# Two graph attention layers on one core: when the four logits of a step end in the order's model, and layer 0's products in parts of two key blocks

## The chip, the core and the metric

The kernel runs on one core of a Trainium2 chip. The time is device time in microseconds of one execution. A profile is one more execution, taken by the hardware profiler.

## The reference

x holds 16 graphs of 1024 nodes with 256 features, adj their adjacency (0 or 1, about 3% ones). Two layers follow each other; behind each one the result is added to x and normalized row by row.

Layer 0 has 4 heads of 64 features. The reference:

```python
h = jnp.einsum('bnd,hde->bhne', nodes_embed, W)
weight = weight + mask * (e_src[:, :, t, :, None] + e_dst[:, :, t, None, :])
weight = jax.nn.leaky_relu(weight, negative_slope=0.01)
weight = jnp.where(node_adj[:, None] == 0, NEG, weight)
attention = jax.nn.softmax(weight, axis=-1)
dst = jnp.einsum('bhij,bhje->bhie', attention, h) + bias[None, :, None, :]
out = jax.nn.relu(dst) + h          # then a normalization of each head's 64 features
```

Layer 1 has 8 heads of 32 features. Queries, keys and values are all the same normalized rows:

```python
scores = jnp.einsum('bhqd,bhkd->bhqk', qkv, qkv) * scale
masked = jnp.where(mask, scores, -jnp.inf)
attn = jax.nn.softmax(masked, axis=-1)
out = jnp.einsum('bhqk,bhkd->bhqd', attn, qkv)
x = x + out                         # then y = layer_norm(x)
mlp = jax.nn.gelu(y @ W1 + b1, approximate=False) @ W2 + b2
```

## The kernel before

**Two streams and one order.** Layer 0 of a graph and layer 1 of the graph before it share the engines. Each layer is a Python generator (layer0 and layer1, lines 941 to 983) that issues instructions and then yields a number of units of work and the things that it needs next. The loop at lines 1007 to 1023 picks, at each turn, which of the two goes on. What it picks sets the order of the instructions in the queues of TensorE (PE), VectorE (DVE), ScalarE (ACT) and GpSimd (POOL); on the chip each of these queues is worked off in that order. All instructions pass through a helper at line 61, so all of them have that line in the profile, and groups are told apart by the names of their tiles.

**How the loop picks.** A whole layer 0 of a graph is WORK0 = 47 units: 13 for prepare, 2 at the start of attention0, 32 for its products. A whole layer 1 is WORK1 = 138 units: 82 for attention (ATTN1), 56 for the mlp. COURSE says how far layer 0 should be (in graphs, ahead of layer 1's graph) when layer 1 has done so many units: 1.0 at its start, 1.42 at unit 82, 2.0 at unit 128 and after. Layer 0 goes on while it is behind this target. The choice is turned round if the stream that was picked is late by 0.3 us more than the other, as long as layer 0 stays within SLACK = 0.06 graphs (2.8 units) of the target, and no further ahead than 2.05 graphs (lines 1011 to 1016).

**Where lateness comes from.** Class Pace (lines 90 to 167) keeps a model of the chip while the program is built: for each engine when it is free, for each tile when it was last written and read. enter() puts an instruction at the latest of these and adds a cost; a matmul of a 32x128 tile over 512 columns is 0.22 us in it. The four such matmuls of a step start one after the other in the model. written of a tile is the end of its matmul plus 0.2. Ring.ready() gives when the oldest buffers of a ring come free.

**Layer 0.** prepare (line 481) loads two blocks of 128 rows at a time, turns them (tiles xk, xT), turns the adjacency (ak) to a mask of bytes (ACT, Square), and projects (w0e). Since a logit of layer 0 is a sum of a term of the query and one of the key, exp of the leaky sum is a maximum of two products; spread_factor (line 558) spreads the query's term over all partitions with matmuls into two of the four ps banks and copies them to cb by ACT; weights (line 569) makes p0 by one DVE instruction for each key block of 128 keys and 512 queries. products (line 586) multiplies p0 with the values in 128x64 tiles, 8 matmuls for a key block, each with two records in the profile. A step of attention0 is a head, a half of the queries and four of the eight key blocks: 64 records, named acc<-v,p. Its weights are two p0 tiles; ring "four" has four such buffers, and weights of step i+1 are issued behind the products of step i. spread_factor for the next pair of heads is issued in the first step of a pair's second head.

**After layer 0.** residual0 and after0 (lines 626 to 717) are chains: generators that go on in advance() when what they need is ready in the model. after0 normalizes per head, then per row; its ACT instruction sq<-hb,t,r makes the normalized rows, and PE and ACT turn them into nT, that is layer 1's queries and keys.

**Layer 1.** exponentials (line 729) makes a step's four logits: four matmuls of 32x128 tiles (records ps<-nT, eight a step) into the four banks of the ring ps_s, and four exponentials on ACT into two p tiles. masked multiplies them with the mask on DVE. products (line 748) does two heads as "moved" (po<-p,v and po<-p,unit) and two as "held" (po<-v,p), three steps behind the logits (LAG). There are 32 steps a graph. The mlp (line 858) goes over four chunks of 256 rows: first() is ps<-yT,w_sb and a gelu on ACT, second() is po<-w_sb,hid; one unit of the order is two first() or half a second(), 1.75 each.

The step loop of attention0 as it stands:

```python
steps = [(n, hd, j4) for n in range(NH) for hd in range(H0) for j4 in range(0, NB, 4)]
...
            products(ps, hd, j4, av)
            advance()
            if i + 1 < len(steps):
                ps = weights(*steps[i + 1])
```

Of the kernel before, what the change touches and what calls it, by code (L numbers as in the profile page):

```python
# [31 lines left out]
F32 = mybir.dt.float32  # L32
# [4 lines left out]
OP = mybir.AluOpType  # L37
PSUM = bass.MemoryType.PSUM

P = 128  # L40
# [49 lines left out]
class Pace:  # L90
# [20 lines left out]
    def through(self, tile):  # L111
        return max(self.written.get(tile, 0.0), self.read.get(tile, 0.0))

    def now(self):
        return self.free["tensor"]

# [54 lines left out]
def fast_path(  # L171
# [24 lines left out]
    nc = Pace(tc.nc)  # L196
    B, N, D = x.shape
    H0, _, HO = w0.shape
# [4 lines left out]
    NB = N // P  # L203
    DC = D // P
    FC = DFF // P
    HALF = 512
    NH = N // HALF
    BPH = HALF // P
    Q = 32
    TILE = 64  # L210
    PAIR = 2
    GB = 2
    QUAD = 4
# [337 lines left out]
    def attention0(b, hb, v0, esr, dinv, factors, mask, rinv):  # L551

        groups = [(n, pair) for n in range(NH) for pair in range(H0 // PAIR)]
        steps = [(n, hd, j4) for n in range(NH) for hd in range(H0) for j4 in range(0, NB, 4)]

        def spread_factor(n, pair):

            cb = two.tile([P, PAIR, HALF], F32, name="cb")  # L560
            pbs = [ps_s.tile([P, HALF], F32, name="ps") for _ in range(PAIR)]
            for e in range(PAIR):
                q = slice((pair * PAIR + e) * Q, (pair * PAIR + e + 1) * Q)
                nc.tensor.matmul(pbs[e], spread[q, :], esr[q, n * HALF : (n + 1) * HALF], start=True, stop=True)
            for e in range(PAIR):
                nc.scalar.copy(cb[:, e, :], pbs[e])
            return cb

        def weights(n, hd, j4):
            ps = []  # L570
            cb = cbs[n, hd // PAIR]
            for j2 in (j4, j4 + 2):
                p = four.tile([P, 2, HALF], F32, name="p0")
                for i in range(2):
                    nc.vector.scalar_tensor_tensor(
                        p[:, i, :],
                        cb[:, hd % PAIR, :],
                        dinv[:, j2 + i, hd : hd + 1],
                        mask[n][:, j2 + i, :],
                        op0=OP.max,  # L580
                        op1=OP.mult,
                    )
                ps.append(p)
            return ps

        def products(ps, hd, j4, av):
            for i in range(4):
                for q in range(BPH):
                    for at in range(0, P, TILE):
                        nc.tensor.matmul(  # L590
                            av[at : at + TILE, q, :],
                            ps[i // 2][:, i % 2, q * P + at : q * P + at + TILE],
                            v0[:, j4 + i, hd, :],
                            start=j4 + i == 0 and q == 0,
                            stop=j4 + i == NB - 1 and q == BPH - 1,
                        )

        cbs = {groups[0]: spread_factor(*groups[0])}
        yield 1.0,
        nc.vector.tensor_copy(factors, v0[:, :, :, HO])  # L600
        ps = weights(*steps[0])
        yield 1.0, bank0_ready, *ps
        for i, (n, hd, j4) in enumerate(steps):
            if j4 == 0:
                av, bank = bank0([P, BPH, HO + 1])
                bank["busy"] = True
            products(ps, hd, j4, av)
            advance()
            if i + 1 < len(steps):
                ps = weights(*steps[i + 1])  # L610
            if j4 == 0 and i + 3 < len(steps) and hd % PAIR == PAIR - 1:
                g = steps[i + 3][0], steps[i + 3][1] // PAIR
                cbs[g] = spread_factor(*g)
            if j4 == NB - 4:
                h = hb[n][:, :, hd * HO : (hd + 1) * HO]
                residual = residual0(av, h, rinv[:, n * BPH : (n + 1) * BPH, hd])
                residuals[b, n, hd] = residual
                bank["busy"] = False
                bank["readers"] = [residual]
                begin(residual, "vector", av)  # L620
                if hd % PAIR == PAIR - 1:
                    norms[b, n, hd] = after0(b, n, hd, hb[n])
                    begin(norms[b, n, hd], "vector", done(residual), hb[n])
            yield (2.0, *ps, *([bank0_ready] if j4 == NB - 4 else []))

    def residual0(av, h, rinv):

# [92 lines left out]
    def attention1(half, mask, rinv, half_done):  # L720

        steps = [(n, quad, jb) for n in range(NH) for quad in range(H1 // QUAD) for jb in range(NB)]

        def exponentials(n, quad, jb):
            keys = slice(jb % BPH * P, (jb % BPH + 1) * P)  # L730
            of_keys, of_queries = half(jb // BPH)[2], half(n)[2]
            tiles = [ps_s.tile([P, HALF], F32, name="ps") for _ in range(QUAD)]
            for e in range(QUAD):
                q = slice(e * HD, (e + 1) * HD)
                nc.tensor.matmul(tiles[e], of_keys[q, quad, keys], of_queries[q, quad, :], start=True, stop=True)
            ps = []
            for e in range(0, QUAD, PAIR):
                p = eight.tile([P, PAIR, HALF], F32, name="p")
                for i in range(PAIR):
                    nc.scalar.activation(p[:, i, :], tiles[e + i], AF.Exp, scale=SCALE1)  # L740
                ps.append(p)
            return ps

        def masked(n, quad, jb, ps):
            for p in ps:
                nc.vector.tensor_mul(p, p, mask[n][:, jb, None, :].to_broadcast([P, PAIR, HALF]))

        def products(quad, jb, ps, moved, held):
            values = half(jb // BPH)[1][:, jb % BPH, :, :]
            for e in range(PAIR):  # L750
                hd = quad * QUAD + e
                for at, v in ((e, values[:, hd, 0:HD]), (PAIR + e, unit)):
                    nc.tensor.matmul(
                        moved[at * Q : (at + 1) * Q, :], v, ps[0][:, e, :], start=jb == 0, stop=jb == NB - 1
                    )
            for e in range(PAIR):
                hd = quad * QUAD + PAIR + e
                for q in range(BPH):
                    for at in range(0, P, Q):
                        nc.tensor.matmul(  # L760
                            held[at : at + Q, q, e, :],
                            ps[1][:, e, q * P + at : q * P + at + Q],
                            values[:, hd, :],
                            start=jb == 0 and e == 0 and q == 0,
                            stop=jb == NB - 1 and e == PAIR - 1 and q == BPH - 1,
                        )

        LAG = 3
        ready = {}

        def logits_ready():
            return ps_s.ready("ps", QUAD)

        def outs_ready():
            return ps_o.ready("po", 2)

        for i in range(len(steps) + LAG):
            if i < len(steps):
                ready[i] = exponentials(*steps[i])
                advance()  # L780
            if 0 <= i - 1 < len(steps):
                masked(*steps[i - 1], ready[i - 1])
                advance()
            if i < LAG:
                yield 1.0, logits_ready
                continue
            n, quad, jb = steps[i - LAG]
            if jb == 0:
                moved = ps_o.tile([P, HALF], F32, name="po")
                held = ps_o.tile([P, BPH, PAIR, HD + 1], F32, name="po")  # L790
            products(quad, jb, ready.pop(i - LAG), moved, held)
            if jb == NB - 1:
                if quad == 0:
                    o = one.tile([P, BPH, D], F32, name="o0")
                chain = heads_out(n, quad, moved, held, o, rinv)
                begin(chain, "vector", held, moved, o)
                if quad == H1 // QUAD - 1:
                    half_done(n, o, chain)
            yield (2.5, logits_ready, *ready.get(i - LAG + 1, ()), *([outs_ready] if jb == NB - 1 else []))
# [185 lines left out]

    WORK0 = NB // GB * 3.25 + 2.0 + NB * H0 // 2 * 2.0
    ATTN1 = 2.0 + 2.5 * (NH * NB * H1 // QUAD)
    WORK1 = ATTN1 + NB // GB * (1.75 * FC / 2 + 3.5 * GB)  # L990
    SLACK = 0.06
    COURSE = [(0.0, 1.0), (ATTN1, 1.42), (WORK1 - 10.0, 2.0), (WORK1, 2.0)]

    def wanted():
        b, done = place[1]
# [11 lines left out]
    while any(streams):  # L1007
# [9 lines left out]
        step = next(streams[which], None)  # L1017
# [453 lines left out]
```

## Time and profile before

| | us |
|---|---|
| median of 3 runs | 3573.72 (3570.82 to 3583.27) |
| profiled execution | 3564.78 |
| its span, first to last instruction | 3563.0 |
| PE busy | 3443.4 (97%) |
| DVE busy | 2989.8 (84%) |
| ACT busy | 2010.2 (56%) |
| mean granted clock of PE | 0.983 |

The costliest groups, with count, busy us and mean ns: exponentials on ACT (p<-ps, 2048, 1061.0, 616); masking on DVE (p<-p,mask, 1024, 1188.9, 1217); logits on PE (ps<-nT, 4096 records, 794.6, 651); layer 0's weights on DVE (p<-cb,dinv,mask, 1024, 698.9, 743); layer 0's products on PE (acc<-v,p, 16384 records, 547.6, 225). Matmuls overlap in these rows: busy time is the time in which at least one is under way, and their ends are modelled. The distance from the start of one group to the start of the next is what a group takes of PE.

The first graph's layer 0 runs alone until about 115 us, and the last graph's layer 1 runs alone from about 3384 us. Between them a graph takes some 217 us. In the timeline a row is a run of like instructions: start, length, engine, line, operation, tiles, shapes, count, and in brackets the idle time before it with what ended it.

### The profile page before, as it was taken

The numbers are of one execution on the slowest core, as the hardware profiler recorded it, in microseconds if no ns is written. First come the engines' busy times: TensorE is split into PE (matmuls) and PEld (weight loads), VectorE is DVE, ScalarE is ACT, GpSimd is POOL, SyncE is SP. The second block draws the span as 40 slices with busy tenths as digits, with TensorE's granted clock in tenths as the row PEclk, the third lists the DMA queues.
The fourth block names the chain that finished last, engine by engine and source line by source line (L and its number), as shares of the span: only waits on it lengthen the run. The fifth ranks groups of instructions, "written<-read, shape, count | busy, mean of one in ns | idle before, by whom it ended". The sixth has DMA issues, their size and how long they took to land.

```text
span 3563.0 us, 141472 instructions
## 1 busy us (share of the span) xinstructions
PE 3443.4 (97%) x64417; PEld 2329.2 (65%) x64417; DVE 2989.8 (84%) x5267; ACT 2010.2 (56%) x4320; POOL 413.7 (12%) x424
## 2 busy tenths in 40 slices
PE   6799999999999999999999999999999999999998
PEld 4458576675856658576585766757567585765846
DVE  5888898988888888898888979888798888988883
ACT  2564746547375563845647466474654737556373
POOL 0102011010110101011020110101101011010100
PEclk9899999999999999999999999999999999999999
DMA  4111101011020110201111010110201102010000
GB/s 107 32 20 34 30 14 41 12 34 30 16 45 9 37 24 17 47 12 35 21 30 33 13 39 15 34 30 14 41 13 33 30 16 45 9 37 9 16 6 14
DMA packets 77809, 97.51 MB, mean 27 GB/s; under 512 B 9104, under 2 KB 60048, under 8 KB 77200
## 3 DMA queue, kind: packets, MB, share of 16 engines
q0 software_dynamic: 18432, 33.56, 6.4%
q1 hardware_dynamic: 57184, 53.76, 5.0%
q8 instruction: 506, 8.29, 1.0%
q10 hardware_dynamic: 1584, 1.05, 0.1%
q14 instruction: 103, 0.84, 0.1%
HBM read 105.13 MB, written 16.78 MB: 34 GB/s over the span
## 4 chain that ended last, share of the span: by engine, by line
PE 91%; ACT 5%; DVE 2%; issue 1%; DMA 0%; POOL 0%; ACTq 0%; POOLq 0%; DVEq 0%
PE po L61 36%; PE ps L61 34%; PE acc L61 21%; ACT p L61 2%; DVE p L61 1%; ACT sq L61 1%; ACT mask L61 1%; ACT xT L61 0%; ACT z L61 0%; DMA w0e<-in_L_gnn_W_dram 0%; DVE hb L61 0%; ACT cb L61 0%; ACT hb L61 0%; POOL r L61 0%; DVE z L61 0%
## 5 line engine op out<-in xcount | busy, mean ns | idle before, releaser
L61 ACT ACTIVATE p<-ps 128x512 f32<-128x512 f32 x2048 | 1061.0, 616 | 417.3 <-PE ps L61 417.3
L61 DVE TENSOR_TENSOR p<-p,mask 128x1024 f32<-128x1024 f32 x1024 | 1188.9, 1217 | 27.0 <-ACT p L61 26.8
L61 PE MATMUL ps<-nT 32*128 32x512 f32 x4096 | 794.6, 651 | 12.3 <-ACT cb L61 9.8
L61 DVE SCALAR_TENSOR_TENSOR p<-cb,dinv,mask 128x512 f32<-128x512 f32 x1024 | 698.9, 743 | 23.3 <-ACT cb L61 23.3
L61 PEld LDWEIGHTS po<-v,p 128*32 128x32 f32 x32768 | 398.6, 110 | 317.0 <-issue 264.8
L61 ACT ACTIVATE hid<-ps,b_sb 128x256 f32<-128x256 f32 x512 | 242.5, 474 | 639.6 <-PE ps L61 639.6
L61 PE MATMUL acc<-v,p 128*64 128x65 f32 x16384 | 547.6, 225 | 18.3 <-DVE p L61 16.3
L61 PEld LDWEIGHTS acc<-v,p 128*64 128x64 f32 x16384 | 507.9, 139 | 83.6 <-issue 38.8
L61 PE MATMUL po<-p,v 128*32 128x512 f32 x2048 | 553.5, 615 | 0.0
L61 PE MATMUL po<-p,unit 128*32 128x512 f32 x2048 | 553.1, 615 | 0.0
L61 PE MATMUL ps<-yT,w_sb 128*128 128x256 f32 x2048 | 478.4, 383 | 0.0
L61 PE MATMUL po<-w_sb,hid 128*128 128x256 f32 x2048 | 474.6, 384 | 0.0
L61 PEld LDWEIGHTS po<-w_sb,hid 128*128 128x128 f32 x2048 | 381.7, 190 | 64.8 <-issue 11.4
L61 PEld LDWEIGHTS ps<-yT,w_sb 128*128 128x128 f32 x2048 | 380.3, 190 | 62.9 <-issue 11.4
L61 PEld LDWEIGHTS ps<-nT 32*128 32x128 f32 x4096 | 286.2, 186 | 166.2 <-ACT p L61 56.8
L61 PE MATMUL po<-v,p 128*32 128x33 f32 x32768 | 390.5, 198 | 4.4 <-issue 4.4
L61 PEld LDWEIGHTS po<-p,v 128*32 128x32 f32 x2048 | 78.7, 109 | 340.0 <-issue 210.8
L61 POOL TENSOR_TENSOR r<-v,mhalf 128x1 f32<-128x1 f32 (+1 forms) x192 | 152.8, 801 | 842.0 <-DVE v L61 493.0
L61 DVE TENSOR_TENSOR z<-acc,bias_r 128x256 f32<-128x256 f32 x128 | 54.1, 423 | 200.0 <-ACT hb L61 200.0
L61 POOL TENSOR_TENSOR r<-v1s,mhalf 128x4 f32<-128x4 f32 x32 | 61.7, 1927 | 1092.9 <-DVE v1s L61 1092.9
L61 POOL DMA_DIRECT2D ak<-in_adj_dram x128 | 69.7, 545 | 976.9 <-PE acc L61 963.1
L61 PE MATMUL acc<-w0e,xT 128*128 128x264 f32 x512 | 149.3, 415 | 20.0 <-issue 10.4
(109 smaller groups left out, 2909.4 us busy)
## 6 DMA issues: line engine op xcount, KB each, us to landing
ak<-in_adj_dram POOLq DMA_DIRECT2D x128, 256.0 KB, 3.9
xk<-in_x_dram SPq DMA_DIRECT2D x64, 256.0 KB, 2.8
xl<-in_x_dram SPq DMA_DIRECT2D x32, 512.0 KB, 3.9
out_dram<-z SPq DMA_DIRECT2D x128, 128.0 KB, 1.7
w_sb<-in_L_gnn_W_dram SPq DMA_DIRECT2D x2, 1024.0 KB, 6.7
v<-in_L_gnn_a_src_dram SPq DMA_DIRECT2D x2, 320.0 KB, 4.4
v<-in_L_gnn_a_dst_dram ACTq DMA_DIRECT2D x1, 320.0 KB, 6.5
xl<-in_L_gnn_a_dst_dram ACTq DMA_DIRECT2D x1, 320.0 KB, 7.8
```

Source lines behind the costliest of these rows:

```text
L61: return method(*args, **kwargs)
```

## The change

The model gets a method, together(), which sets the model's read and written times of several tiles to the latest among them. exponentials calls it ahead of a step's four logits and behind them. It issues no instruction. Layer 0's products go in parts of two key blocks (32 records) for one unit each, in place of four key blocks for two units; the weights of three parts are made before the first products, and those of part i+3 are issued behind the products of part i. spread_factor for the next pair is issued in the first part of a pair's second head, four parts ahead of the first that belongs to the next pair. COURSE asks for 1.38 in place of 1.42 at the end of attention, and for 2.0 from 14 units before the end, in place of 10. WORK0 stays 47.

```diff
--- before.py
+++ after.py
@@ -110,6 +110,12 @@
 
     def through(self, tile):
         return max(self.written.get(tile, 0.0), self.read.get(tile, 0.0))
+
+    def together(self, tiles):
+
+        names = [t.tensor.name for t in tiles]
+        for times in (self.read, self.written):
+            times.update(dict.fromkeys(names, max(times.get(name, 0.0) for name in names)))
 
     def now(self):
         return self.free["tensor"]
@@ -208,6 +214,7 @@
     BPH = HALF // P
     Q = 32
     TILE = 64
+    AHEAD = 3
     PAIR = 2
     GB = 2
     QUAD = 4
@@ -553,7 +560,7 @@
 
 
         groups = [(n, pair) for n in range(NH) for pair in range(H0 // PAIR)]
-        steps = [(n, hd, j4) for n in range(NH) for hd in range(H0) for j4 in range(0, NB, 4)]
+        steps = [(n, hd, j) for n in range(NH) for hd in range(H0) for j in range(0, NB, PAIR)]
 
         def spread_factor(n, pair):
 
@@ -566,52 +573,50 @@
                 nc.scalar.copy(cb[:, e, :], pbs[e])
             return cb
 
-        def weights(n, hd, j4):
-            ps = []
+        def weights(n, hd, j):
             cb = cbs[n, hd // PAIR]
-            for j2 in (j4, j4 + 2):
-                p = four.tile([P, 2, HALF], F32, name="p0")
-                for i in range(2):
-                    nc.vector.scalar_tensor_tensor(
-                        p[:, i, :],
-                        cb[:, hd % PAIR, :],
-                        dinv[:, j2 + i, hd : hd + 1],
-                        mask[n][:, j2 + i, :],
-                        op0=OP.max,
-                        op1=OP.mult,
-                    )
-                ps.append(p)
-            return ps
-
-        def products(ps, hd, j4, av):
-            for i in range(4):
+            p = four.tile([P, PAIR, HALF], F32, name="p0")
+            for i in range(PAIR):
+                nc.vector.scalar_tensor_tensor(
+                    p[:, i, :],
+                    cb[:, hd % PAIR, :],
+                    dinv[:, j + i, hd : hd + 1],
+                    mask[n][:, j + i, :],
+                    op0=OP.max,
+                    op1=OP.mult,
+                )
+            return p
+
+        def products(p, hd, j, av):
+            for i in range(PAIR):
                 for q in range(BPH):
                     for at in range(0, P, TILE):
                         nc.tensor.matmul(
                             av[at : at + TILE, q, :],
-                            ps[i // 2][:, i % 2, q * P + at : q * P + at + TILE],
-                            v0[:, j4 + i, hd, :],
-                            start=j4 + i == 0 and q == 0,
-                            stop=j4 + i == NB - 1 and q == BPH - 1,
+                            p[:, i, q * P + at : q * P + at + TILE],
+                            v0[:, j + i, hd, :],
+                            start=j + i == 0 and q == 0,
+                            stop=j + i == NB - 1 and q == BPH - 1,
                         )
 
         cbs = {groups[0]: spread_factor(*groups[0])}
         yield 1.0,
         nc.vector.tensor_copy(factors, v0[:, :, :, HO])
-        ps = weights(*steps[0])
-        yield 1.0, bank0_ready, *ps
-        for i, (n, hd, j4) in enumerate(steps):
-            if j4 == 0:
+
+        ps = [weights(*step) for step in steps[:AHEAD]]
+        yield 1.0, bank0_ready, ps[0]
+        for i, (n, hd, j) in enumerate(steps):
+            if j == 0:
                 av, bank = bank0([P, BPH, HO + 1])
                 bank["busy"] = True
-            products(ps, hd, j4, av)
+            products(ps.pop(0), hd, j, av)
             advance()
-            if i + 1 < len(steps):
-                ps = weights(*steps[i + 1])
-            if j4 == 0 and i + 3 < len(steps) and hd % PAIR == PAIR - 1:
-                g = steps[i + 3][0], steps[i + 3][1] // PAIR
-                cbs[g] = spread_factor(*g)
-            if j4 == NB - 4:
+            if i + AHEAD < len(steps):
+                ps.append(weights(*steps[i + AHEAD]))
+            if j == 0 and i + NB // PAIR < len(steps) and hd % PAIR == PAIR - 1:
+                n1, hd1, _ = steps[i + NB // PAIR]
+                cbs[n1, hd1 // PAIR] = spread_factor(n1, hd1 // PAIR)
+            if j == NB - PAIR:
                 h = hb[n][:, :, hd * HO : (hd + 1) * HO]
                 residual = residual0(av, h, rinv[:, n * BPH : (n + 1) * BPH, hd])
                 residuals[b, n, hd] = residual
@@ -621,7 +626,7 @@
                 if hd % PAIR == PAIR - 1:
                     norms[b, n, hd] = after0(b, n, hd, hb[n])
                     begin(norms[b, n, hd], "vector", done(residual), hb[n])
-            yield (2.0, *ps, *([bank0_ready] if j4 == NB - 4 else []))
+            yield (1.0, *ps[:1], *([bank0_ready] if j == NB - PAIR else []))
 
     def residual0(av, h, rinv):
 
@@ -730,9 +735,12 @@
             keys = slice(jb % BPH * P, (jb % BPH + 1) * P)
             of_keys, of_queries = half(jb // BPH)[2], half(n)[2]
             tiles = [ps_s.tile([P, HALF], F32, name="ps") for _ in range(QUAD)]
+
+            nc.together(tiles)
             for e in range(QUAD):
                 q = slice(e * HD, (e + 1) * HD)
                 nc.tensor.matmul(tiles[e], of_keys[q, quad, keys], of_queries[q, quad, :], start=True, stop=True)
+            nc.together(tiles)
             ps = []
             for e in range(0, QUAD, PAIR):
                 p = eight.tile([P, PAIR, HALF], F32, name="p")
@@ -985,11 +993,11 @@
 
 
 
-    WORK0 = NB // GB * 3.25 + 2.0 + NB * H0 // 2 * 2.0
+    WORK0 = NB // GB * 3.25 + 2.0 + NB * H0 * 1.0
     ATTN1 = 2.0 + 2.5 * (NH * NB * H1 // QUAD)
     WORK1 = ATTN1 + NB // GB * (1.75 * FC / 2 + 3.5 * GB)
     SLACK = 0.06
-    COURSE = [(0.0, 1.0), (ATTN1, 1.42), (WORK1 - 10.0, 2.0), (WORK1, 2.0)]
+    COURSE = [(0.0, 1.0), (ATTN1, 1.38), (WORK1 - 14.0, 2.0), (WORK1, 2.0)]
 
     def wanted():
         b, done = place[1]
```

## The prediction

> **What bounds the kernel now.** I first read the page's head: TensorE (PE) is busy 97% of the span, VectorE (DVE) 84%, ScalarE (ACT) 56%.
>
> ```profile
> span 3563.0 us, 141472 instructions
> PE 3443.4 (97%) x64417; PEld 2329.2 (65%) x64417; DVE 2989.8 (84%) x5267; ACT 2010.2 (56%) x4320; POOL 413.7 (12%) x424
> ...
> PE 91%; ACT 5%; DVE 2%; issue 1%; DMA 0%; POOL 0%; ACTq 0%; POOLq 0%; DVEq 0%
> ```
>
> The chain of waits agrees: PE 91%. But 97% isn't PE at its peak. So second I read the timeline of one graph in the middle of the run (1643 to 1861 us; others look alike) and took, for each group of matmuls, the distance to the start of the next. A logits step (8 records of ps<-nT, four matmuls of 32 rows side by side) usually takes 1.07 us:
>
> ```profile
> 1668.62 1.14 PE L61 MATMUL ps<-nT 32*128 32x512 f32 x8
> 1669.69 0.62 PE L61 MATMUL po<-p,v 128*32 128x512 f32 x1
> ...
> 1669.77 2.06 ACT L61 ACTIVATE p<-ps 128x512 f32<-128x512 f32 x4 [1.20 <-PE ps L61]
> ...
> 1671.24 1.77 PE L61 MATMUL ps<-nT 32*128 32x512 f32 x8
> ...
> 1672.94 0.62 PE L61 MATMUL po<-p,v 128*32 128x512 f32 x1
> ```
>
> The step at 1668.62 is over at 1669.69. The next starts 2.62 us later, while ACT works on the exponentials of the first until 1671.83; two of its four banks are not free, its matmuls go two by two, and it takes 1.70 (to 1672.94). The step is shown busy, and 0.63 us are lost in it. I counted all 512 steps so: 232 us over 1.07 each. For the 14 graphs between the first and the last this is, per graph: 4.8 us in the first four steps, 4.4 in **bare** steps (7 of 10 that follow the products of layer 1 with nothing of layer 0 between lose 0.63), 3.6 beside the two spread_factor calls that fall among logits (they take two of the four ps banks; the second makes one step take 3.3), 1.0 behind the transposes for the mlp, and 0.5 elsewhere: 14.3, or 200 in all. The first graph loses 14, and the last 18 with no layer 0 left to fill it.
>
> Third, the stages of that graph:
>
> ```profile
> 1643.20:1662.10 18.90, 17.19 (x144) 9.11 (x143) 15.33 (x40) 16.24 (x39) 3.72 (x5) 0.85 0.36 84
> 1662.10:1766.00 103.90, 103.04 (x2484) 56.12 (x2480) 89.38 (x116) 75.04 (x165) 5.15 (x7) 0.99 0.14 26
> 1766.00:1861.00 95.00, 94.81 (x1406) 79.57 (x1404) 81.47 (x174) 34.25 (x67) 16.93 (x14) 1.00 0.05 16
> ```
>
> The columns are length, busy PE, PEld, DVE, ACT, POOL, then the granted clock. The first row is the passage from one graph to the next: ACT is busy 16.24 of 18.90 us there, and the clock is 0.85. The usual durations of what PE does in it add up to 10.2 us (four logits 4.28, products 1.56, two input projections 1.98, transposes 2.39), so some 8.7 us are lost. ACT has four rounds of exponentials, two masks, the four rows of the normalization, nT:
>
> ```profile
> 1651.15 2.18 ACT L61 ACTIVATE sq<-hb,t,r 128x256 f32<-128x256 f32 x4
> ...
> 1654.48 0.66 PE L61 MATMUL acc<-ident,sq 128*128 128x128 f32 x4 [1.44 <-ACT mask L61]
> ```
>
> **The change part by part.** No arithmetic, tile size, DMA or ring is added; all four edits act through the order in which the queues are filled. Its terms are per graph, times the 15 graphs that have layer 0 beside them.
>
> *A, bare steps.* Before, the model lets the four matmuls run one after the other, 0.22 us each, so it thinks the first exponential starts 0.22+0.2 after the step begins and the banks are free 0.66 us earlier than if all four end together. The trace says together (0.63 lost). With `together` the model sees a bare step as late by about 0.5 us, over its bound of 0.3, and takes a part of layer 0 where SLACK allows one. It will not get more of layer 0: COURSE gives 0.38*47 = 17.9 units in attention, not 19.7. What it can do is split fillers that stand together now (both a turn of the mask and a projection behind one step) and put a part of 1.0 where 2.0 stood. I take 4 of 7 late bare steps away: 4 x 0.63 = 2.5 us, 38 in all. Bounds: 0, if SLACK is always used up, and 4.4 (66 in all).
>
> *B, spread_factor.* The second of a graph is issued with the fifth part, that is at 15+5 = 20 units; COURSE and SLACK allow 17.9+2.8 = 20.7 by the end of attention. So it comes at the end or in the mlp, where sp4 costs 1.06 as now and no logits wait. 2.25 us of one step at 0.6: 1.3, 20 in all (bounds 0 and 3.6, or 54).
>
> *C, the passage.* Layer 0 is to be done 14 units before the end of layer 1, not 10. A unit of the mlp is some 1.05 us (1.83 for 1.75), so its last products come 4.2 us earlier than now, at 8.8 us before the passage:
>
> ```profile
> 1632.36 2.09 PE L61 MATMUL acc<-v,p 128*64 128x65 f32 x64
> 1634.37 1.99 PE L61 MATMUL ps<-yT,w_sb 128*128 128x256 f32 x8
> 1636.20 7.07 PE L61 MATMUL po<-w_sb,hid 128*128 128x256 f32 x32
> 1643.20 1.14 PE L61 MATMUL ps<-nT 32*128 32x512 f32 x8
> ```
>
> The chain behind it (residual, two sums, two powers on POOL, bias at 1648.4) then ends near 1644, and the 2.18 us of sq can stand in the 5 us in which ACT idles before the first exponential. That takes 2.2 from the 16.24 that ACT has there: 2.2 us, 33 in all. Bounds: 0 (sq still behind the exponentials) and 8.7 (130 in all). Its input load xl goes out 4 us earlier on SP's queue, which has nothing behind it but outputs; 3.9 us to land, hidden as now.
>
> *D, more changes of the array's shape in the mlp.* Here the change costs. A part of four key blocks (64 records) takes 2.02 us, of which 32 pairs at 59 ns are 1.89 and entry and exit 0.13. Its neighbours pay as well: second-layer halves beside it take 1.82 against 3.45/2 = 1.73, first-layer pairs 1.83 against 1.72. Now one part stands behind every second unit (1609.69, 1615.36, 1621.02, 1626.69, 1632.36: 5.67 us apart). Target then rises by 0.62/42*1.75*47 = 1.2 units for each unit of the mlp, so a part of 1.0 goes behind nearly each. Two units with one long part: 3.65+2.02 = 5.67. With two short ones: 2 x 1.925 + 2 x (0.94+0.13) = 5.99. That is 0.33 for each of some 11 added interruptions: 3.6 us, 54 in all. Bounds: 0 (always two in a row) and 16 x 0.33 = 5.3 (79 in all). [...] The trace has 0.33 in the mlp and less in attention.
>
> *E, in attention* a part between held products and logits costs its 0.13 alone; two more a graph, 0.3, 4 in all.
>
> *Weights three parts ahead.* The DVE instructions are the same 1024. Buffer (i+3) mod 4 is that of part i-1, whose products stand before those of part i on PE, so no new wait on the ring. At a head start 6 instead of 4 weights (4.1 against 2.7 us) stand before layer 1's masks on DVE; products lag three steps behind logits, which leaves two steps (5.3 us) of cover. Without it, 1.4 us once a graph (21 in all). spread_factor now has one part of 1.07 us, not 2.02, before the first weight that reads cb; the copies can be late by 1 to 2 us on DVE, whose weights are three parts ahead for PE: nothing, at most 4 x 1 us a graph (60 in all) if masks then come late. What it could bring is small: PE waits for these weights 16 us in all, in the first graph, where DVE is busy 55.86 of 57.00 us and stays the bound.
>
> Sum: -38 -20 -33 +54 +4 = **-33 us**. The profiled execution took 3564.8 us (span 3563.0); -33 makes 3532. The median of the runs shown is 3573.7, 9 above it; the same difference makes **3541**.
>
> **The rivals.**
> *Slower: the interruptions decide.* D is certain, since COURSE forces layer 0 into 42 units of mlp; A to C depend on where an order made greedily happens to fall. If SLACK is used up, as it is behind the passage now (bare steps at 1662, 1665, 1668 follow layer 0 having run ahead), A and B are 0 and C a half: 58-16 = +42, 3616; with A to C at a third, +28, 3602. It decides from less than 58/15 = 3.9 us gained a graph. For it: 14 of the 32 logits steps of a graph lose time, but the fillers among them don't grow in number.
> *Same:* gains of 48 to 68 against 58: within 0.3% (11 us, what a measurement here can tell from no change). That is also the case in which the model's new lateness changes nothing that matters.
> *Much faster: the passage closes.* The granted clock of 0.85 over the passage is 2.8 of its 18.9 us; if the chain is through before the first logits, that may go as well. [...] With C at 6, A at 4 and B at 2.5 a graph: -188+58 = -130, 3444. Against it: ACT still has 14 us of work for 10 us of PE.
>
> **How the numbers follow.** Forecast (3510 to 3563) 0.42; faster than that 0.2; same (3563 to 3584) 0.13; slower 0.25. So faster by over 0.3% is 0.62. The range leaves out the best of the third case and the worst of the first: 3480 to 3605.
>
> **What would show it.** Right: logits steps over 1.07 us lose under 190 us in all, not 232; in the middle graphs fewer than 7 bare steps of 1.70; no step of 3.3 with a spread inside; sq before the passage's second logits; the passage under 17.5 us; the mlp stage longer by 3 to 4 us than 95.0 for as many key blocks, with acc<-v,p in groups of 32 between units. Wrong: groups of 64 still, bare steps as many as now, or PE waiting for p0 or cb in attention.

## The result

| | before | after |
|---|---|---|
| median of all runs shown, us | 3573.41 (10 runs, 3564.2 to 3583.27) | 3565.43 (10 runs, 3563.28 to 3570.58) |
| profiled execution, us | 3564.78 | 3565.24 |
| mean granted clock of PE in it | 0.983 | 0.974 |
| clock halved in it, us in all | 123 | 187 |
| logits steps over 1.07 us, lost in all | 232 | 143 |
| groups of layer 0's products on PE | 247 | 412 |

The ratio after to before is 0.9979 (95% interval 0.9967 to 0.9990): 8 us faster, within the 11 us that the prediction called no change. It had 33. The two profiled executions are equal; that of before lies 9 us under its median. So the profiles, and the sums below, explain this equal pair. Other runs of before go from 3559 us at a granted clock of 0.985 to 3585 us at 0.977, so the 8 us between the medians may lie in the clock; that is not shown.

### The profile page after: what moved, and what is told of

It reads as the page before. It is cut to its first block, busy times and chain, and to the rows that moved or that the text cites. A ratio compares the mean times of both kernels' runs of the same rounds, so it can differ in the third digit from the quotient of the medians.

```text
span 3563.4 us, 141495 instructions
## 1 busy us (share of the span) xinstructions
PE 3446.7 (97%) x64417; PEld 2301.0 (65%) x64417; DVE 2984.4 (84%) x5267; ACT 2010.3 (56%) x4320; POOL 416.4 (12%) x424
## 4 chain that ended last, share of the span: by engine, by line
PE 84%; DVE 8%; ACT 4%; issue 2%; DMA 1%; POOL 0%; POOLq 0%; ACTq 0%; DVEq 0%
PE po L61 32%; PE ps L61 31%; PE acc L61 22%; DVE p L61 7%; ACT p L61 2%; ACT sq L61 1%; DVE x L61 1%; ACT mask L61 1%; ACT z L61 0%; DMA w0e<-in_L_gnn_W_dram 0%; DVE hb L61 0%; ACT oT L61 0%; DMA xl<-in_L_gnn_a_dst_dram 0%; ACT o L61 0%; ACT xT L61 0%
## 5 line engine op out<-in xcount | busy, mean ns | idle before, releaser
L61 PE MATMUL ps<-nT 32*128 32x512 f32 x4096 | 715.5, 666 | 1.5 <-ACT p L61 1.5
L61 DVE SCALAR_TENSOR_TENSOR p<-cb,dinv,mask 128x512 f32<-128x512 f32 x1024 | 710.9, 743 | 0.7 <-ACT cb L61 0.7
L61 PEld LDWEIGHTS acc<-v,p 128*64 128x64 f32 x16384 | 525.1, 140 | 129.2 <-issue 68.4
L61 PE MATMUL acc<-v,p 128*64 128x65 f32 x16384 | 585.7, 227 | 19.9 <-DVE p L61 12.3
L61 PE MATMUL po<-w_sb,hid 128*128 128x256 f32 x2048 | 490.6, 387 | 0.0
L61 PE MATMUL ps<-yT,w_sb 128*128 128x256 f32 x2048 | 487.1, 386 | 0.0
L61 PE MATMUL po<-v,p 128*32 128x33 f32 x32768 | 386.8, 198 | 12.1 <-DVE o L61 10.2
L61 PEld LDWEIGHTS ps<-nT 32*128 32x128 f32 x4096 | 241.9, 190 | 121.5 <-issue 50.6
L61 ACT COPY cb<-ps 128x512 f32<-128x512 f32 x128 | 68.8, 589 | 254.7 <-PE ps L61 254.7
```

The source lines that it names most:

```text
L61: return method(*args, **kwargs)
```

## The profile after

The page's head and the shares of the chain of waits:

```profile
span 3563.4 us, 141495 instructions
PE 3446.7 (97%) x64417; PEld 2301.0 (65%) x64417; DVE 2984.4 (84%) x5267; ACT 2010.3 (56%) x4320; POOL 416.4 (12%) x424
...
PE 84%; DVE 8%; ACT 4%; issue 2%; DMA 1%; POOL 0%; POOLq 0%; ACTq 0%; DVEq 0%
```

Nothing in the first two lines tells the kernels apart. In the chain, DVE's share rises from 2% to 8% and PE's falls from 91% to 84%, but PE still carries it. Two groups of the page do tell (busy us, mean ns, idle before with its releaser):

```profile
L61 PE MATMUL ps<-nT 32*128 32x512 f32 x4096 | 715.5, 666 | 1.5 <-ACT p L61 1.5
...
L61 PE MATMUL acc<-v,p 128*64 128x65 f32 x16384 | 585.7, 227 | 19.9 <-DVE p L61 12.3
```

The logits hold PE 79 us less than before (794.6), the products of layer 0 38 more (547.6), for the same instructions. The stages show where: the same graph in the middle of the run, cut at its first logits, its fifth logits and its first mlp matmul (columns: length, busy PE, PEld, DVE, ACT, POOL, granted clock, DMA):

```profile
1644.80:1662.10 17.30, 15.01 (x141) 8.79 (x140) 12.67 (x33) 15.80 (x35) 3.59 (x5) 0.80 0.39 80
1662.10:1770.70 108.60, 107.83 (x2805) 58.88 (x2805) 96.80 (x127) 79.32 (x174) 5.11 (x7) 1.00 0.14 25
1770.70:1860.20 89.50, 89.50 (x1086) 74.18 (x1084) 76.32 (x170) 30.31 (x61) 17.29 (x14) 1.00 0.06 19
```

I did this for all graphs between the first and the last. A key block of layer 0 is 0.47 us of PE (8 pairs of records at 59 ns), so stages with unequal shares of layer 0 are compared "at 20" key blocks in attention and "at 44" in the mlp, as before has them:

| mean of 14 graphs, us | before | after | difference |
|---|---|---|---|
| passage (first four logits steps) | 18.3 | 18.4 | +0.1 |
| attention (key blocks) | 115.3 (20) | 109.0 (14) | |
| attention at 20 | 115.3 | 111.8 | -3.4 |
| mlp (key blocks, groups) | 83.6 (44, 11) | 89.4 (50, 20) | |
| mlp at 44 | 83.6 | 86.6 | +3.0 |

That is -0.3 us a graph, -4 in all. The start gained 2 (second graph's layer 1 from 344.1 to 342.3 us), the last graph, alone, lost 6 (179.3 to 185.5): its passage fell into a stretch of 13.7 us at half clock and one more of its steps takes 3.75. Attention gained and the mlp gave it back; the passage, which was to bring the sum, didn't move.

*Attention.* Steps of 1.70 with nothing of layer 0 before them fell from 7 to 3 a graph, and the fillers stand one by one:

```profile
1691.44 2.06 ACT L61 ACTIVATE p<-ps 128x512 f32<-128x512 f32 x4 [1.10 <-PE ps L61]
...
1693.00 0.62 PE L61 MATMUL acc<-identb,ak 128*128 128x128 bf16 x8
1693.55 1.14 PE L61 MATMUL ps<-nT 32*128 32x512 f32 x8
...
1694.62 0.62 PE L61 MATMUL po<-p,v 128*32 128x512 f32 x1
```

The turn of a mask at 1693.00 fills the 0.55 us until the banks are free, and the logits at 1693.55 take 1.07.

*Mlp.* The parts of 32 records stand between nearly all units:

```profile
1783.98 1.99 PE L61 MATMUL po<-w_sb,hid 128*128 128x256 f32 x8
1785.90 1.15 PE L61 MATMUL acc<-v,p 128*64 128x65 f32 x32
1786.99 1.99 PE L61 MATMUL po<-w_sb,hid 128*128 128x256 f32 x8
1788.91 2.09 PE L61 MATMUL acc<-v,p 128*64 128x65 f32 x64
```

From start to start a half of a second() takes 1.92 here (1783.98 to 1785.90), where two in a row took 3.45.

*Passage.* Layer 0's last products end at 1632.5, 12.3 us before the passage, not 8.8. The rows (sq) come 4.0 us after its first logits, where they came 7.9 after. That is still inside:

```profile
1645.96 2.07 ACT L61 ACTIVATE p<-ps 128x512 f32<-128x512 f32 x4 [4.03 <-PE ps L61]
...
1646.91 2.29 PE L61 MATMUL ps<-nT 32*128 32x512 f32 x8
...
1647.07 0.15 DVE L61 SCALAR_TENSOR_TENSOR t<-mv,r 128x4 f32<-128x4 f32 x1
...
1648.85 2.10 ACT L61 ACTIVATE sq<-hb,t,r 128x256 f32<-128x256 f32 x4
...
1652.58 1.01 PE L61 MATMUL acc<-identb,ak 128*128 128x128 bf16 x8 [2.29 <-ACT mask L61]
...
1656.53 1.95 PE L61 MATMUL acc<-ident,sq 128*128 128x128 f32 x8
1657.74 2.07 ACT L61 ACTIVATE nT<-acc,be_c,g_c 128x256 f32<-128x256 f32 x4
```

The rows' last input (t) is there at 1647.2, behind the second logits' start, and ACT does the rows soon behind the first exponentials; so a mask comes later, and PE waits 2.29 us for its bank. The clock halves for 6.8 us of the passage (0.80 over it); the transposes of the rows take 1.88 from start to start.

*A new wait.* Each graph has one step where layer 1 goes on to its second four heads and needs the banks of the first:

```profile
1741.84 4.62 DVE L61 TENSOR_TENSOR p<-p,mask 128x1024 f32<-128x1024 f32 x4
...
1746.61 0.42 DVE L61 TENSOR_TENSOR o<-po,ranges 128x256 f32<-128x256 f32 x1
...
1747.18 0.76 PE L61 MATMUL po<-v,p 128*32 128x33 f32 x64 [0.67 <-DVE o L61]
```

DVE reads the bank behind four masks. Before, a part of 2.02 us stood ahead of this step's logits and covered it; now one of 1.08 doesn't, and the held products start 1.28 us behind the last of the moved ones, not 0.42: 0.86 us a graph, 13 in all.

## The experiments

Times are medians of each kernel's runs, beside runs of before on the same chip (3573 to 3581 from chip to chip); so a few us between kernels say little. This table has the stages of all, and the text below follows from it:

| kernel | us | passage | attention at 20 | mlp at 44 | groups in the mlp |
|---|---|---|---|---|---|
| before | 3573 | 18.3 | 115.3 | 83.6 | 11 |
| after | 3565 | 18.4 | 111.8 | 86.6 | 20 |
| e1_together | 3592 | 17.7 | 116.3 | 84.8 | 13 |
| e2_parts | 3639 | 19.0 | 113.9 | 88.8 | 25 |
| e3_course | 3638 | 18.0 | 119.7 | 84.0 | 12 |
| e4_no_together | 3680 | 18.9 | 119.3 | 86.6 | 20 |
| e7_old_course | 3647 | 18.5 | 114.7 | 89.1 | 25 |
| f1_together_course | 3531 | 19.2 | 110.2 | 85.1 | 13 |
| f2_ahead2 | 3562 | 18.9 | 110.3 | 87.3 | 22 |
| e5_pairs | 3513 | 14.4 | 114.6 | 84.3 | 14 |
| e6_early | 3497 | 14.3 | 111.5 | 86.5 | 18 |
| e8_rows_dve | 3516 | 14.8 | 112.1 | 86.7 | 20 |
| r9_before_early | 3591 | 14.2 | 114.8 | 89.4 | 11 |
| r10_early_pairs | 3527 | 13.4 | 111.6 | 89.3 | 14 |
| r11_early18 | 3556 | 17.1 | 112.2 | 86.6 | 21 |
| r12_early_rows | 3510 | 15.3 | 111.8 | 85.8 | 18 |
| f3_tc_rows | 3543 | 16.8 | 110.4 | 87.8 | 13 |

**Which edit does what.** The three edits are together(), the parts (of two key blocks, weights three ahead), and COURSE. All eight combinations were run.

e1_together is before with the method and its two calls:

```diff
+            nc.together(tiles)
             for e in range(QUAD):
...
+            nc.together(tiles)
```

> The kernel before with together() alone: parts of four key blocks, weights one step ahead and COURSE as before. Theory (the model's view of the logits is what takes the stalls away, the short parts only cost): the loss of logits steps over 1.07 us falls from 232 to about 170 us, groups of layer 0's products stay near 247, the mlp stage stays at 83.6 us a graph, and the time falls by 20 to 40 us, to 3535 to 3553. Rival (the shorter parts and the smaller share of layer 0 in attention take them away): logits still lose over 210 us and the time is within 10 us of before.

3591.88 us, ratio 1.0045 (1.0027 to 1.0062): slower. The bare steps' loss fell (61 to 36 us in the 14 graphs), but the logits lose 210 in all, and PE waits anew at the change of heads (a line of this kernel's waits of PE):

```profile
PE po L61 <- DVE ranges L61: 37.7, 15, 2.7
PE acc L61 <- DVE z L61: 36.0, 22, 2.2
```

The three numbers are us in all, times and the longest. The second wait takes 8.5 us in before. Neither theory holds: the model's correction alone moves layer 0 so that DVE is late elsewhere.

e2_parts is after without together() and with before's COURSE.

> The kernel before with parts of two key blocks and weights three parts ahead alone; no together(), COURSE as before. Theory: over 380 groups of layer 0's products, 0.33 us for each added one in the mlp (the stage 2.5 to 3.5 us longer a graph for as many key blocks), logits lose 200 to 232 us as before, so 30 to 50 us slower than before, 3600 to 3620. Rival: the logits' loss falls below 180 us with the short parts alone, and the time is within 15 us of before.

3638.81, 1.0170 (1.0141 to 1.0200). The mlp pays 5.2 us at 44 for 14 more groups, 0.37 each; the theory had a price of 0.33 and 2.5 to 3.5 us, that is fewer groups, and a time of 3600 to 3620. The logits lose 186, less than it had and more than the rival's 180.

e3_course changes one line:

```diff
-    COURSE = [(0.0, 1.0), (ATTN1, 1.42), (WORK1 - 10.0, 2.0), (WORK1, 2.0)]
+    COURSE = [(0.0, 1.0), (ATTN1, 1.38), (WORK1 - 14.0, 2.0), (WORK1, 2.0)]
```

> The kernel before with the new COURSE alone. Theory (the passage between graphs is bound by ScalarE's work and not by the chain behind layer 0): key blocks move from attention to the mlp, the passage stays at 18 to 19 us, the time is within 12 us of before (3562 to 3585). Rival (the chain sets the passage): it takes under 17 us a graph and the time falls by 25 us or more.

3637.76, 1.0158 (1.0124 to 1.0193). The passage stays, as expected; the time doesn't: attention is 4.4 us longer at 20, some 62 us over 14 graphs.

e4_no_together is after without the two calls.

> The kernel after without together(). Theory: logits lose over 200 us again, not 143, the interruptions of the mlp stay at 20 a graph, and the time is 30 to 60 us over that of after, 3595 to 3625. Rival (together changes little): within 10 us of after, 3555 to 3576.

3680.49, 115 us over after, where 30 to 60 were expected; the logits lose 188 in all, less than expected. Two waits on this kernel's PE take more:

```profile
PE acc L61 <- DVE z L61: 69.8, 38, 3.5
PE ps L61 <- ACT p L61: 34.9, 16, 2.3
```

In e3 and e4 the last projections of prepare stand in a bunch (15 times, once a graph, a turn of the mask takes 4.1 us between two projections; in after never), and PE's wait for z on DVE goes with it (98.2 us in e3, 69.8 in e4). With this COURSE together() takes 7.5 us a graph off attention (119.3 to 111.8), far beyond the bare steps. With the old COURSE it adds 1.0 (before to e1).

e7_old_course is after with before's COURSE.

> The kernel after with COURSE as before (1.42 and 10 units): together() and the short parts alone. Theory (the gain of attention needs together() and short parts, COURSE only moves key blocks): attention at equal key blocks within 1.5 us of after, the time within 15 us of after. Rival (COURSE is fitted to this order, another value of it gives a bunch of turned masks that wait): attention 3 to 5 us a graph longer at equal key blocks and the time 40 us or more over after.

3647.10, 82 us over after: nearly the rival, whose time it has. Attention is 2.9 us longer, just short of its 3 to 5, and the mlp, which neither had, is 2.5 longer (25 groups). The rival's bunch of projections is not there: no turn of a mask takes 4.1 us between two projections. So it is COURSE together with together() that gains in attention; either alone adds to it.

f1_together_course is before with together() and the new COURSE.

> The kernel before with together() and the new COURSE, parts of four key blocks: the one combination of the three edits not yet run. Theory (with together() the gaps are seen, and it is the short part that fits them): attention at equal key blocks stays 2 us or more a graph over that of after, the mlp has 11 to 13 groups, and the time is 3575 to 3610. Rival (together() with this COURSE is enough, short parts only cost): attention as in after, and 20 us or more under after.

3531.11, ratio 0.9883 (0.9845 to 0.9921). My theory falls. Attention at 20 is 110.2, even 1.6 under after, with parts of four key blocks; the mlp has 13 groups. The short parts aren't what fits the gaps: beside the other two edits they cost 34 us (3531 to 3565; by the two ratios to before 0.0096, the same).

f2_ahead2 is after with `AHEAD = 2`.

> The kernel after with the weights two parts ahead, that is four key blocks as before, not six. Theory (DVE's weights are not late for PE in after, so the third part ahead changes nothing but the order): PE waits for p0 under 20 us in all, the time is within 15 us of after. Rival (the third part is what keeps layer 0's products from waiting at a spacing of one unit): PE waits over 40 us for p0 and the time is 25 us or more over after.

3562.08, as after. PE waits as little for p0:

```profile
PE acc L61 <- DVE p L61: 14.7, 10, 2.2
```

The third part ahead has no share that can be seen in the time. But the stages differ: the new wait at the change of heads is not there, attention at 20 is 1.5 us shorter, the passage and the mlp are 0.5 and 0.7 longer.

**The interruptions.** e5_pairs keeps two parts together in the mlp:

```diff
+        owed = 0.0
         for i, (n, hd, j) in enumerate(steps):
...
-            yield (1.0, *ps[:1], *([bank0_ready] if j == NB - PAIR else []))
+            owed += 1.0
+            if i % 2 == 1 or place[1][1] < ATTN1:
+                yield (owed, *ps[:1], *([bank0_ready] if j == NB - PAIR else []))
+                owed = 0.0
```

> The kernel after, but while layer 1 is in its mlp layer 0 gives two parts of two key blocks in a row without a turn between (one step of two units); in attention single parts stay. Theory (each added group of layer 0's products in the mlp costs 0.3 us of PE by changes of the array's shape): groups fall from 20 to 11 or 12 a graph, the mlp stage from 89.4 to 86.5 us, attention stays at 109, the time falls by 35 to 50 us to 3515 to 3530. Rival (the stage is longer for another reason, or the order gives it back in attention): within 12 us of after.

3513.21, 52 us under after, just past the expected 35 to 50, and for another reason: the mlp at 44 gave 2.3 us a graph for 6 groups, attention took 2.8 back, and the passage fell from 18.4 to 14.4. So this run doesn't give the price. The table does: over its first twelve kernels the mlp at 44 goes with the groups at 0.35 us each (a straight line through all; none is over 0.7 us off it). My 0.33 from two rows of before was near. That it is the change of the array's shape that costs was my reading: no run parts it from whatever else an added group brings.

**The passage.** e6_early puts 24 in place of after's 14 units in COURSE.

> The kernel after with layer 0 wanted ready 24 units before the end of layer 1, not 14. Theory (in the passage ScalarE's work is the bound, and at 14 the rows, 2.1 us, and nT, 2.1 us, still fall into it): with the chain 10 us earlier they leave it, and the passage of 18.4 us falls to 14 or 15 us; the mlp stage is as long as before but for the moved key blocks; 30 to 50 us faster than after. Rival (the loop of logits and exponentials with nothing to multiply sets the passage): it stays over 17.5 us and the time within 12 us of after.

e8_rows_dve leaves after's order and makes the rows on DVE:

```diff
-        yield "scalar", t
+        yield "vector", t
         normed = one.tile(rowwise, F32, name="sq")
-        scale_shift(normed, o, t, r2, BPH)
+        for g in range(BPH):
+            nc.vector.tensor_scalar(
+                normed[:, g, :], o[:, g, :], r2[:, g : g + 1], t[:, g : g + 1], op0=OP.mult, op1=OP.add
+            )
```

> The kernel after with the normalized rows of layer 1's input (sq<-hb,t,r, four instructions for each half) made on VectorE and not on ScalarE. Theory (ScalarE bounds the passage): the passage falls by about 2 us a graph from 18.4, and the time by 20 to 35 us. Rival (the loop or VectorE bounds it): the passage stays within 0.7 us, the time within 12 us of after.

Both theories hold in their cause, and both gains are larger than they had: 3497.19 (ratio to before 0.9770, 0.9754 to 0.9787), 68 us under after, and 3515.72 (0.9823, 0.9807 to 0.9840), 50 under. The passage of e6_early, then of e8_rows_dve:

```profile
1615.50:1629.80 14.30, 13.87 (x139) 7.76 (x138) 11.40 (x23) 14.27 (x34) 1.62 (x3) 1.00 0.48 93
```

```profile
1626.40:1641.20 14.80, 14.53 (x141) 8.28 (x140) 12.73 (x31) 13.60 (x31) 3.67 (x5) 1.00 0.39 73
```

With the chain out of the way ACT is busy 14.27 of 14.30 us: the passage is ACT's work, end to end. Taking about 2 us from ACT gives 3.6, and the clock, 0.80 in after's passage, then stays at 1.00. In the middle of the run (300 to 3350 us) it is halved for 113 us in after, 10 in e6 and 3 in e8. How much of the gain is ACT's work and how much the clock isn't parted by a run. An estimate: three passages of before's profile, in which the clock stayed up, took 16.4 us, so of the 4 us some 2 are work and 2 the clock.

r11_early18 has 18 units.

> The kernel after with layer 0 wanted ready 18 units before the end. Theory: the chain is 4 us earlier than at 14, the rows leave the passage and nT does not; ScalarE has 2.1 us less in it, and since less idling keeps the clock up it falls at once to 15 or 16 us: 30 to 50 us faster than after. Rival (it shortens in proportion): 17 us, 15 to 25 us faster.

3555.63, 10 us under after and so less than either had. The passage of 17.1 is the rival's. It ranges from 16.7 to 18.0; the clock still halves in 13 of the 14, so that less idling keeps it up is not shown by this run. PE waits there for xT on ACT:

```profile
PE acc L61 <- ACT xT L61: 31.7, 14, 2.3
```


r12_early_rows has 24 units and the rows on DVE.

> The kernel after with 24 units and the normalized rows made on VectorE. Theory: at 24 units the rows are out of the passage already, so taking them off ScalarE gives nothing more there: passage 14 to 14.6 us, time within 10 us of 3497. Rival (ScalarE's load matters in the whole graph): 15 us or more faster than 3497.

3510.21, 13 over e6_early, and a passage of 15.3: neither number of the theory holds. The rows have nothing more to give there, as it had it, but the order that results has a passage 1.0 us longer.

r9_before_early is before with 24 units.

> The kernel before with layer 0 wanted ready 24 units before the end of layer 1 in place of 10, nothing else. Theory (the passage is bound by ScalarE, whatever the rest of the order): it falls from 18.3 us to 14 to 15 us and the clock is not halved in the middle graphs; with the stages as they are the time falls by 30 to 60 us, to 3515 to 3548. Rival (long parts keep layer 0 late, so that the chain still ends in the passage): it stays over 17 us, the time within 12 us of before.

The passage falls to 14.2, as expected, with the old parts and model. The time is 3591.34: the mlp is 5.8 us a graph longer with the same 11 groups. For 2.9 us of that PE waits for the weights of long parts that follow each other closely; 1.0 is the transposes of the rows, which now stand in the mlp; and the clock is halved there for 2.7 us a graph, where in before it never was. The wait, in the whole run:

```profile
PE acc L61 <- DVE p L61: 58.1, 39, 4.3
```

r10_early_pairs is e6_early with the pairs of e5.

> The kernel after with layer 0 ready 24 units before the end, and two parts in a row in the mlp. The passage has no more to give here, so this is the price of the interruptions by itself. Theory: groups of layer 0's products fall from 18 to 12 to 14 in the mlp, at 0.37 us each the stage is 1.5 to 2.2 us shorter for as many key blocks, and the time 15 to 30 us under the one with 24 units alone (3497), if attention keeps its order. Rival (attention gives it back, as it did with pairs at 14 units): within 8 us of 3497 or above.

3526.59, 29 over e6_early: the rival, for another reason than it had. Attention stays; the mlp at 44 is 89.3 with 14 groups, and DVE is late again:

```profile
PE acc L61 <- DVE p L61: 43.8, 38, 3.1
```

In the mlp this is 2.1 us a graph, none in e6. Fewer groups don't pay here, with DVE late for the weights of two parts in a row.

f3_tc_rows is f1_together_course with the rows on DVE.

> The kernel before with together(), the new COURSE, parts of four key blocks, and the normalized rows made on VectorE: the two findings together. Theory (short parts only cost, and the passage is ScalarE's): passage from 19.2 to about 15 us, attention and mlp as with together() and COURSE alone (3531), so 40 to 60 us less: 3471 to 3491, under the best so far (3497). Rival (with long parts the passage stays long, or VectorE is late in the mlp): passage over 17 us, time over 3510.

3543.29: the rival, by its second reason. The passage falls by 2.4 to 16.8, and the mlp grows by 2.7, 1.9 of it in the same wait for weights (14.5 us in the whole run of f1):

```profile
PE acc L61 <- DVE p L61: 43.5, 24, 4.3
```

The two gains don't add up. e6_early is the fastest of all, 68 us under after and 2.3% under before; it is after with one number changed.

## Why the prediction was wrong

*A, bare steps: right in size, wrong in one reason.* 4 of 7 late steps went (4.4 to 1.9 us a graph). together() with COURSE does it; "put a part of 1.0 where 2.0 stood" isn't needed (f1_together_course).

*B, spread_factor: right.* The second of a graph now stands behind the last logits. The logits gained 2.3, and sp4 (the four matmuls of spread_factor) costs 1.06 by itself now, which ran beside logits before: 1.2, where I had 1.3.

*Not forecast, and gained:* 0.8 us a graph behind the transposes for the mlp.

*C, the passage: the step that failed.* "The 2.18 us of sq can stand in the 5 us in which ACT idles before the first exponential." That idle time ends 1.2 us behind the passage's start (1643.20), in before as in after:

```profile
1644.36 2.06 ACT L61 ACTIVATE p<-ps 128x512 f32<-128x512 f32 x4 [5.36 <-PE ps L61]
```

The prediction's chain, ending "near 1644", left a few tenths of it for 2.18 us of sq, so the step failed by its own numbers. sq came 3.9 us earlier, but it had stood 7.9 us behind the passage's start; to end before the first exponentials it would have had to come 9 us earlier. The sign "sq before the passage's second logits" failed with it: 1648.85 against 1646.91. I had put the chain's end at 1644 from the end of products alone. They came 3.5 us earlier, not 4.2; the square of hb on ACT came 4.1 us behind them, not 2.7, because gelus stood before it; DVE's sums of hb came behind a z (output rows of layer 1) and its sums; and ACT's queue had a z and xT before sq. 33 us were expected and none came. That ACT sets the passage was right (e6_early, e8_rows_dve), and so was that the clock might go as well: the true prize was 4 us a graph, which 14 units don't reach and 24 do.

*D, the interruptions: right.* 9 more groups at 0.33 are 3.0 us a graph, as measured; 11 groups were expected. *E* was right as far as it can be seen.

*Not forecast, and lost:* the wait at the change of heads, 0.86 us a graph. I asked what the longer queue of weights would delay on DVE and looked at products alone, not at the two divisions that free their banks. And 6 us in the last graph.

So A, B, D and E were a wash by themselves (-2.5 -1.2 +3.0 +0.3, -0.8 unforeseen, +0.9 unforeseen: -0.3 us a graph), as they were in the forecast (-38 -20 +54 +4: 0), and the whole forecast gain was C. My rivals had the case ("gains of 48 to 68 against 58: within 0.3%") at 0.13. What stays open is why the new COURSE has the bunch of projections without together() and not with it; that follows from the loop's choices, and no run shows them one by one.

## What to carry to other kernels

When an order is made from a model, its edits don't add up: here each edit alone was slower, and two of the three together were the best of the eight. Before counting on a chain being moved off a busy stretch, work out when its last instruction starts against the start of that stretch, through every queue it passes; here sq came 3.9 us earlier where 9 were needed, and the passage was no shorter. Work that was cut finer paid for each added group (0.35 us in the mlp), and work that was packed closer waited for the engine that feeds it (2.1 us a graph in the mlp of r10_early_pairs, 2.9 in that of r9_before_early); look at both before choosing a size.

## What the runs showed of the hardware

The clock halved in passages in which no single wait of PE was over 2.3 us: in after's passage the longest is 2.29 us, and 6.8 us or 10.2 us at half clock go with it in all 14 graphs; in before's the longest is 1.44 us, and the clock halves in 11 of 14, for 3.4 to 10.1 us. With no wait over 0.28 us in the passage (e6_early, e8_rows_dve) the clock stayed up in all 14. Before shows both states of one and the same passage: 16.4 us in three graphs in which the clock stayed up, and 18.0 to 19.0 in the other eleven, with the same instructions.
